# A decoder layer with routed experts on one core: the split of the groups into phases, the order of the attention units, and the dependencies of the result loads

## The chip, the cores and the metric

The kernel runs on one NeuronCore of one Trainium2 chip. The metric is the device time of one execution in microseconds (us). The profile is one execution taken by the hardware profiler. Engines are named as in its rows: PE (TensorE), PEld (TensorE weight loads), DVE (VectorE), ACT (ScalarE), POOL (GpSimd), SP (SyncE, which here only issues DMAs). "SPq" is SP's instruction queue.

## The reference

Input: `x` and `ctx_1024`, both [32, 128, 128] in float32 (32 sequences, 128 tokens, width 128), 16 heads of 8. One decoder layer:

```python
x = _layernorm(x + _attn(x, x, x, sa_..., True), ln1_g, ln1_b)        # causal self attention
x = _layernorm(x + _attn(x, enc, enc, ca_..., False), ln2_g, ln2_b)   # cross attention
x = _layernorm(x + _moe(x, router_w, router_b, e_w1, e_b1, e_w2, e_b2), ln3_g, ln3_b)
```

`_moe` takes the softmax of 8 router logits for each of the 4096 tokens, keeps the best two, softmaxes those two probabilities again, and adds the two experts' outputs with these weights. An expert is 128 -> 512, exact GELU, 512 -> 128.

## The kernel before, in words

**Groups and units.** The 32 sequences form 8 groups of G = 4. A unit is one sequence's self attention ("s") or cross attention ("c"), so there are 64. The list `order` (from L986) runs them in one software pipeline: 12 s units lead (LEAD), then c and s alternate, then 12 c units end it. Each unit takes two half-slots of its own and is spread over the next six: scores and row maxima (L456, L464), transposed scores and exponentials (L449, L472), values (L511), outputs (L525 to L530).

**The planner.** Everything else that a group needs is cut into generators that stop at `yield`: projections, normalisation (L323), hand-over to cross attention, `keep_x2`, `route` (L607), `place` and `biases`. From L1066 on each step gets a half-slot by hand-written costs (`ROUTE`, `PLACE`, `NORM`); `chain(lo, hi, ...)` puts steps into the least loaded half-slot of an interval and crams what is left into its last ones. The table is then played half-slot by half-slot, and each engine runs its instructions in that order.

**Routing.** `route` computes the logits (L614), subtracts the row maximum (L619), takes the exponential on ACT (L620), finds the best two (L629, L632), and takes a tanh on ACT (L637). `place` gives every token two rows in the table `xs` of its phase, sorted by expert into blocks of 128. `scatter` sends rows: one indirect DMA on POOL for one sequence and one choice (L760), 8 for a group, one for each half-slot; for the last group one for every second half-slot.

**Phases and blocks.** `PHASES` (L25) splits the groups: a phase's blocks can start when all its groups have been scattered. A phase of n groups has 8 blocks with a fixed expert and (1024 n - 8) // 128 whose expert is known at run time: 47 blocks for five groups and 31 for three, 78 in all. The blocks start at half-slot `max(behind, ready)`: `behind` is the end of the attention, 132, and `ready` the end of the first phase's scatters. From then on one half-slot of what is left in the table is played beside each block (`beside`). By the planner's rules, before: group 4 is scattered in half-slots 122 to 129, group 5 in 136 to 143 (blocks 4 to 11), group 6 in 144 to 151, group 7 in every second one from 152 to 166 (blocks 20 to 34). With a limit of h2 + 14 for the last group of the first phase, six of its seven projection and normalisation steps stand in half-slot 109, and nine steps of the last s group stand in half-slot 111.

**A block** (`Pipeline.run`, L928): SP loads the weights of the block four ahead (L825 or L829, 514 KB, five buffers); PE does the first layer (L864, 8 instructions), then the second layer of the block before (L880, 8 instructions); ACT does four GELUs (L869); DVE copies the result to `ot` (L885, four buffers); POOL scatters it into `eo` by an indirect DMA (L887). Every four blocks SP fetches a quad of rows (L812), PE transposes it (L841), DVE copies it (L856). The first quad of the second phase is fetched when the quad before is turned and waits for all scatters of that phase.

**Results.** `combine` (L948) of a group needs the scatters of the first 15, 23, 31, 39 or 47 blocks of its phase (`needed`) and starts four blocks later: at blocks 19, 27, 35 and 43 of the first phase and block 4 of the second for its five groups, at 19 and 27 of the second phase, and after the last block. It loads the base (L953) and the results `gt` (L955) on SP, yields twice (one yield is one block), adds with weights on DVE (L968), normalises and stores (L981). Two groups can be in work at a time. The line `for j in phases[p].done[: needed(...)]` ties the load to the scatters it needs. Whatever else wrote `eo` before the load in program order is tied to it as well, because the tile framework sees one tensor; and every later scatter is tied to the load. `tc.declare_no_dep` takes such a tie away, and is used between the scatters.

Of the kernel before, what the change touches and what calls it, by code (L numbers as in the profile page):

```python
# [21 lines left out]
FF = 512  # L22
NFC = FF // P
G = 4
PHASES = ((0, 5), (5, 3))  # L25
NP = len(PHASES)
NS = E

# [10 lines left out]
VS = 2 * VW  # L39
NPART = 3  # L40
LEAD = 12

TAG = P
XW = P + 2
# [8 lines left out]
def bc(ap, axis, n):  # L53

    ap = ap.unsqueeze(axis)
    shape = list(ap.shape)
    shape[axis] = n
    return ap.broadcast_to(shape)
# [3 lines left out]
def kernel(  # L62
# [35 lines left out]
    B = x.shape[0]  # L98
    NG = B // G
# [32 lines left out]
    groups = {(kind, gi): Group(kind, gi) for kind in "sc" for gi in range(NG)}  # L132
# [109 lines left out]
    lng, lnb, lngT, lnbT, later = [], [], [], [], {}  # L242
# [364 lines left out]
    def route(gr):  # L607


        gi = gr.gi  # L610
        bs = slice(G * gi, G * gi + G)
        pl = mm_tile([P, G, E], f"pl_{gi}")
        for b in range(G):
            nc.tensor.matmul(pl[:, b, :], lhsT=gr.x2T[:, b, :], rhs=rw, start=True, stop=True)  # L614
        lg = small.tile([P, G, E], F32, tag="lg", name=f"lg_{gi}")
        nc.vector.tensor_tensor(lg, pl, bc(rb, 1, G), ALU.add)
        lm = small.tile([P, G], F32, tag="lm", name=f"lm_{gi}")
        nc.vector.tensor_reduce(lm, lg, AX.X, ALU.max)
        nc.vector.tensor_tensor(lg, lg, bc(lm, 2, E), ALU.subtract)  # L619
        nc.scalar.activation(lg, lg, AF.Exp)  # L620
        yield
        ls = small.tile([P, G], F32, tag="ls", name=f"ls_{gi}")
        nc.vector.tensor_reduce(ls, lg, AX.X, ALU.add)
        nc.vector.reciprocal(ls, ls)
        nc.vector.tensor_tensor(lg, lg, bc(ls, 2, E), ALU.mult)
        top = small.tile([P, G, E], F32, tag="top", name=f"top_{gi}")
        idx = small.tile([P, G, E], U32, tag="idx", name=f"idx_{gi}")
        for b in range(G):
            nc.vector.max(top[:, b, :], lg[:, b, :])  # L629
        yield  # L630
        for b in range(G):
            nc.vector.max_index(idx[:, b, :], top[:, b, :], lg[:, b, :])  # L632


        ex = small.tile([P, G], F32, tag="ex", name=f"ex_{gi}")
        nc.vector.tensor_tensor(ex, top[:, :, 0], top[:, :, 1], ALU.subtract)
        nc.scalar.activation(ex, ex, AF.Tanh, scale=0.5)  # L637
        yield
        idf = small.tile([P, G, 2], F32, tag="idf", name=f"idf_{gi}")
        nc.vector.tensor_copy(idf, idx[:, :, 0:2])  # L640
        nc.vector.tensor_copy(gr.x2[:, :, TAG + 1], idf[:, :, 0])
        gr.onehot = small.tile([P, 2, G, E], F32, tag="onehot", name=f"onehot_{gi}", bufs=2)
        for k in range(2):
            nc.vector.tensor_tensor(
                gr.onehot[:, k], bc(later["iota_e"], 1, G), bc(idf[:, :, k], 2, E), ALU.is_equal
            )
        gr.chosen = small.tile([P, G, E], BF16, tag="chosen", name=f"chosen_{gi}", bufs=2)
        nc.vector.tensor_tensor(gr.chosen, gr.onehot[:, 0], gr.onehot[:, 1], ALU.add)
        yield
        nc.vector.tensor_scalar(wts[:, 0, bs], ex, 0.5, 0.5, ALU.mult, ALU.add)  # L650
        nc.vector.tensor_scalar(wts[:, 1, bs], ex, -0.5, 0.5, ALU.mult, ALU.add)


    class Phase:
# [4 lines left out]


        def __init__(self, p):
            self.p, self.sent, self.done, self.first = p, [], [], True

    phases = [Phase(p) for p in range(NP)]

# [130 lines left out]
    class Blocks:  # L796
# [76 lines left out]
        def second_layer(self, i):  # L873
            if i < 0:
                return
            q, p = i // XB, self.ph.p
            w, h = self.w.pop(i), self.h.pop(i)
            po = mm_tile([P, P], f"po_{p}_{i}")
            for c in range(NFC):
                nc.tensor.matmul(  # L880
                    po, lhsT=h[:, c, :], rhs=w[:, W2 + c * P : W2 + (c + 1) * P],
                    start=c == 0, stop=c == NFC - 1,
                )
            ot = moe.tile([P, P], F32, tag="ot", name=f"ot_{p}_{i}", bufs=4)
            nc.vector.tensor_copy(ot, po)  # L885
            nc.gpsimd.memset(apart, 0.0)
            s = nc.gpsimd.indirect_dma_start(  # L887
                out=eo[p][:, :],
                out_offset=bass.IndirectOffsetOnAxis(
                    ap=self.to[q][:, i % XB : i % XB + 1], axis=0  # L890
                ),
                in_=ot, in_offset=None,
            )
            for j in self.ph.done:
                tc.declare_no_dep(s.ins, j.ins, reason="rows of their own")
            self.ph.done.append(s)

# [46 lines left out]
    def needed(n):  # L944

        return NS + 2 * G * (n + 1) - 1

    def combine(gr):  # L948

        p = next(p for p, (g0, n) in enumerate(PHASES) if gr.gi < g0 + n)  # L950
        first = FREE[p] + 2 * P * G * (gr.gi - PHASES[p][0])
        gr.acc = moe.tile([P, G, P], F32, tag="acc", name=f"acc_{gr.gi}")
        nc.sync.dma_start(out=gr.acc, in_=x2d[gr.gi])  # L953
        gt = act.tile([P, 2, G, 2 * P], F32, tag="qb", name=f"gt_{gr.gi}", bufs=4)[:, 0]
        i = nc.sync.dma_start(  # L955
            out=gt,
            in_=eo[p][first : first + 2 * P * G, :].rearrange(
                "(p b k) d -> p b (k d)", p=P, k=2
            ),
        )  # L960
        for j in phases[p].done[: needed(gr.gi - PHASES[p][0])]:
            tc.add_manual_dep(i.ins, j.ins.name, SYNC, reason="results")
        yield
        yield
        for k in range(2):
            for b in range(G):
                t = G * gr.gi + b
                nc.vector.scalar_tensor_tensor(  # L968
                    gr.acc[:, b, :], gt[:, b, P * k : P * k + P], wts[:, k, t : t + 1],
                    gr.acc[:, b, :], ALU.mult, ALU.add,  # L970
                )
            yield
        yield from finish(gr)
# [9 lines left out]
        )  # L983


    order = []  # L986
    for j in range(B + LEAD):
        if j >= LEAD:
            order.append(("c", j - LEAD))
        if j < B:  # L990
            order.append(("s", j))
    units = [Unit(groups[kind, j // G], j % G) for kind, j in order]
    where = {(kind, j): t for t, (kind, j) in enumerate(order)}
    table = {}
# [1 line left out]
    def at(h, *call):  # L996
        table.setdefault(h, []).append(call)
        return h + 1
# [27 lines left out]
    def chain(lo, hi, *parts):  # L1026


        todo = []
        for made, *costs in parts:  # L1030
            if len(costs) == 1:
                todo.append((costs[0], (made,)))
                continue
            steps = []

            def step(made=made, steps=steps):
                if not steps:
                    steps.append(made())
                next(steps[0], None)

            todo += [(cost, (step,)) for cost in costs]
        ends = []
        for n, (cost, call) in enumerate(todo):
            left = len(todo) - 1 - n
            end = book(lo, hi - left, cost, *call)
            lo = end if hi - end + 1 >= left else end - 1
            ends.append(end)
        return ends

    def pe(us, act=0.0, dve=0.0):  # L1050
        return us, dve, act, 0.0

    def dve(us, act=0.0):
        return 0.0, us, act, 0.0
# [4 lines left out]
    NORM = (dve(1.2), (0.0, 0.9, 0.0, 1.3), dve(0.2), dve(0.0, 0.7), dve(0.0, 0.7))  # L1059
    TURN = (pe(0.45, 0.4),) * 2  # L1060
    PROJECT = (pe(0.45, 0.0, 0.4),) * 2
    ROUTE = (pe(0.3, 0.1, 0.9), dve(1.2), dve(1.1), dve(0.8), dve(0.4))
    PLACE = (pe(0.2, 0.0, 1.0), pe(0.3, 0.0, 0.8), dve(1.6), dve(0.8), dve(0.6))
    behind = 2 * (len(units) + 2)
    sent = 0
    for gi in range(NG):  # L1066
        s, c = groups["s", gi], groups["c", gi]
        h0, h3 = 2 * where["s", G * gi], 2 * where["s", G * gi + G - 1]
        h1, h2 = 2 * where["c", G * gi], 2 * where["c", G * gi + G - 1]
        if gi > 1:  # L1070
# [24 lines left out]
        )  # L1095
        chain(h1 - 1, h1 + 4, (lambda c=c: values_of(c), *TURN))
        ends = chain(
            h2 + 9, h2 + (14 if gi == PHASES[0][1] - 1 else 18),
            (lambda c=c: turn_output(c), *TURN),
            (lambda c=c: project(c), *PROJECT, *NORM),  # L1100
            (lambda c=c: keep_x2(c), *TURN, pool(1.3), pool(1.4)),
        )
        ends = chain(ends[10], ends[10] + 4, (lambda c=c: route(c), *ROUTE))
        ph = phases[next(p for p, (g0, n) in enumerate(PHASES) if gi < g0 + n)]
        ends = chain(ends[-1], ends[-1] + 4, (lambda c=c, ph=ph: place(c, ph), *PLACE))
        h = ends[3]
        chain(h, h + 5, (lambda c=c: biases(c), dve(0.6), pe(0.1, 0.3), pe(0.45, 0.0, 0.6), pool(0.0)))

        h, far = max(h, sent), 1 + (gi == NG - 1)
        for b in range(G):  # L1110
            for k in range(2):
                at(h, scatter, c, ph, b, k)
                h += far
        sent = h
        if gi == PHASES[0][1] - 1:
            ready = h
# [5 lines left out]

    blocks = Pipeline(*(Blocks(ph) for ph in phases))
    start = max(behind, ready)
    at(start - 3, blocks.prepare)
    at(start - 1, blocks.first_rows)

    def unit(t):
# [125 lines left out]
```

## Time and profile before

| | us |
|---|---|
| three runs | 720.62, 730.99, 732.46 (median 730.99) |
| the profiled execution | 720.12 |
| its span | 718.4 |
| attention, to the first block's first layer (L864) | 0 to 477.3 |
| blocks 0 to 77, to the end of the last second layer | 477.3 to 692.7 |
| tail | 692.7 to 718.4 |

Busy over the span: PE 594.3 us (83%), PEld 500.2, DVE 416.3, ACT 403.4, POOL 367.2. Such a share is an average over the two parts; what binds is read part by part. In a line of the timeline the first number is the start, the second the length, `xN` the number of instructions merged, and the bracket the idle time of the engine before it and what ended that. A line of waits has the total, the number of times and the longest. A line of the windows has, after the stretch, the busy time (and instructions) of PE, PEld, DVE, ACT and POOL, the granted PE clock (1.00 is full), the busy share of the 16 DMA engines and GB/s.

### The profile page before, as it was taken

The numbers are of one execution on the slowest core, as the hardware profiler recorded it, in microseconds if no ns is written. First come the engines' busy times: TensorE is split into PE (matmuls) and PEld (weight loads), VectorE is DVE, ScalarE is ACT, GpSimd is POOL, SyncE is SP. The second block draws the span as 40 slices with busy tenths as digits, with TensorE's granted clock in tenths as the row PEclk, the third lists the DMA queues.
The fourth block names the chain that finished last, engine by engine and source line by source line (L and its number), as shares of the span: only waits on it lengthen the run. The fifth ranks groups of instructions, "written<-read, shape, count | busy, mean of one in ns | idle before, by whom it ended". The sixth has DMA issues, their size and how long they took to land. (4 is left out here: it accounts for less than half of the span.)

```text
span 718.4 us, 21892 instructions
## 1 busy us (share of the span) xinstructions
PE 594.3 (83%) x8810; PEld 500.2 (70%) x8863; DVE 416.3 (58%) x1321; ACT 403.4 (56%) x919; POOL 367.2 (51%) x747
## 2 busy tenths in 40 slices
PE   8787999999897987987987888998986697699750
PEld 6565677777775776766776667777885697599750
DVE  2555465656786777678678577436674424353343
ACT  4455666776764683684576554354843454266441
POOL 3274654544446636646554453514886565265350
PEclk9999999999998998998999899759998988799985
DMA  5012516400000200100100000415996889699851
GB/s 133 19 33 64 86 44 192 170 4 17 16 3 17 62 2 14 50 2 24 35 21 6 13 30 10 156 60 173 302 296 227 265 291 313 228 353 346 274 181 59
DMA packets 48038, 82.48 MB, mean 115 GB/s; under 512 B 7968, under 2 KB 26464, under 8 KB 47936
## 3 DMA queue, kind: packets, MB, share of 16 engines
q1 hardware_dynamic: 42816, 71.57, 31.6%
q0 software_dynamic: 4544, 9.38, 3.6%
q8 instruction: 69, 1.13, 0.6%
q14 instruction: 33, 0.27, 0.1%
q10 hardware_dynamic: 576, 0.13, 0.1%
HBM read 62.15 MB, written 23.10 MB: 119 GB/s over the span
## 5 line engine op out<-in xcount | busy, mean ns | idle before, releaser
L869 ACT ACTIVATE h<-ph,wd 128x128 f32<-128x128 f32 x312 | 88.9, 369 | 86.4 <-PE ph L864 46.6
L887 POOL DMA_INDIRECT eo<-ot,to x78 | 78.1, 1001 | 98.3 <-DMA gt<-eo 34.9
L864 PE MATMUL ph<-xT,wd 128*128 128x128 f32 x624 | 93.2, 297 | 32.6 <-DMA wd<-wpk 12.5
L464 DVE TENSOR_REDUCE m_s<-sc_s 128x8 f32<-128x1024 f32 x64 | 78.3, 1223 | 67.1 <-PE st_s L449 59.1
L476 POOL TENSOR_SCALAR_AFFINE_SELECT pr_s<-pr_s 128x1024 f32<-128x1024 f32 x64 | 70.1, 1095 | 86.3 <-ACT pr_s L472 86.1
L864 PEld LDWEIGHTS ph<-xT,wd 128*128 128x128 f32 x624 | 84.4, 210 | 37.4 <-DVE xT L856 15.0
L464 DVE TENSOR_REDUCE m_c<-sc_c 128x8 f32<-128x1024 f32 x64 | 78.3, 1223 | 46.4 <-PE st_c L449 28.8
L472 ACT ACTIVATE pr_s<-st_s 128x1024 f32<-128x1024 f32 x64 | 65.8, 1028 | 65.0 <-PE st_s L449 64.9
L472 ACT ACTIVATE pr_c<-st_c 128x1024 f32<-128x1024 f32 x64 | 65.8, 1029 | 60.7 <-PE st_c L449 58.1
L456 PE MATMUL sc_c<-k_c,qb_c 32*128 32x128 f32 x1024 | 80.1, 297 | 14.0 <-DVE m_s L464 9.0
L880 PE MATMUL po<-wd,h 128*128 128x128 f32 x624 | 87.8, 286 | 1.1 <-ACT h L869 1.1
L880 PEld LDWEIGHTS po<-wd,h 128*128 128x128 f32 x624 | 81.1, 202 | 1.8 <-ACT h L869 1.5
L449 PE MATMUL st_c<-qb_c,k_c 32*128 32x128 f32 x1024 | 77.8, 291 | 0.0
L456 PEld LDWEIGHTS sc_c<-k_c,qb_c 32*128 32x128 f32 x1024 | 67.0, 198 | 15.3 <-DVE m_s L464 9.6
L449 PEld LDWEIGHTS st_c<-qb_c,k_c 32*128 32x128 f32 x1024 | 76.2, 205 | 0.9
L456 PE MATMUL sc_s<-k_s,qb_s 32*128 32x128 f32 x1024 | 74.2, 283 | 0.3
L760 POOL DMA_INDIRECT xs<-x,slots x64 | 64.4, 1007 | 12.0 <-issue 12.0
L449 PEld LDWEIGHTS st_s<-qb_s,k_s 32*128 32x128 f32 x1024 | 67.7, 187 | 0.0
L449 PE MATMUL st_s<-qb_s,k_s 32*128 32x128 f32 x1024 | 67.4, 270 | 0.0
L456 PEld LDWEIGHTS sc_s<-k_s,qb_s 32*128 32x128 f32 x1024 | 62.1, 185 | 1.7 <-issue 1.3
L885 DVE COPY ot<-po 128x128 f32<-128x128 f32 x78 | 22.5, 288 | 60.1 <-PE po L880 46.6
L441 PEld LDWEIGHTS <-ones 32*128 32x128 bf16 x256 | 14.8, 91 | 56.8 <-issue 54.8
(243 smaller groups left out, 1220.1 us busy)
## 6 DMA issues: line engine op xcount, KB each, us to landing
wd<-wpk SPq DMA_DIRECT2D x78, 514.0 KB, 5.4
xt<-xs SPq DMA_DIRECT2D x20, 260.0 KB
wpk<-in_L_xattn_e_w_dram SPq DMA_DIRECT2D x16, 256.0 KB, 6.4
gt<-eo SPq DMA_DIRECT2D x8, 512.0 KB
xs<-blank SPq DMA_DIRECT2D x1, 3120.0 KB
xs<-blank SPq DMA_DIRECT2D x1, 2080.0 KB
xg<-in_x_dram SPq DMA_DIRECT2D x8, 256.0 KB, 3.2
eg<-in_ctx_dram SPq DMA_DIRECT2D x8, 256.0 KB, 7.2
```

The costliest lines, as they stand in the source:

```text
L441: nc.tensor.matmul(st[:, i], lhsT=ones16[rowsof(g), :], rhs=old.mq[rowsof(g)], start=True, stop=False,)
L449: nc.tensor.matmul(st[:, i, r, :], lhsT=old.group.k[rowsof(g), old.b, :], rhs=old.group.qb[rowsof(g), old.b, r, :], start=False, stop=r == 3,)
L456: nc.tensor.matmul(sc[:, i, r, :], lhsT=new.group.qb[rowsof(g), new.b, r, :], rhs=new.group.k[rowsof(g), new.b, :], start=not new.masked, ...
L464: nc.vector.tensor_reduce(new.m[:, 8 * half : 8 * half + 8], sc.rearrange("p i r k -> p (i r) k"), AX.X, ALU.max,)
L472: nc.scalar.activation(old.pr[:, hs, :], st.rearrange("p i r k -> p (i r) k"), AF.Exp, scale=SCALE)
L476: nc.gpsimd.affine_select(out=old.pr[:, hs, :], in_=old.pr[:, hs, :], pattern=[[0, 8], [1, P]], compare_op=ALU.is_ge, fill=0.0, base=0, ch ...
L760: i = nc.gpsimd.indirect_dma_start(out=xs[ph.p][:, :], out_offset=bass.IndirectOffsetOnAxis(ap=slots[:, k, t : t + 1], axis=0), in_=gr.x2[ ...
L864: nc.tensor.matmul(hid[:, c, :], lhsT=w[:, c * P : (c + 1) * P], rhs=self.xT[i // XB][:, i % XB, :], start=True, stop=True,)
L869: nc.scalar.activation(self.h[i][:, c, :], hid[:, c, :], AF.Gelu, bias=w[:, B1 + c : B1 + c + 1])
L880: nc.tensor.matmul(po, lhsT=h[:, c, :], rhs=w[:, W2 + c * P : W2 + (c + 1) * P], start=c == 0, stop=c == NFC - 1,)
L885: nc.vector.tensor_copy(ot, po)
L887: s = nc.gpsimd.indirect_dma_start(out=eo[p][:, :], out_offset=bass.IndirectOffsetOnAxis(ap=self.to[q][:, i % XB : i % XB + 1], axis=0), i ...
```

## The change

- Phases of four and four groups instead of five and three: 39 and 39 blocks, still 78.
- The order of units: at s units 16, 20 and 24 no c unit is put in between, so that self attention runs up to 15 units ahead and 15 c units end the list.
- The limit h2 + 14 becomes h2 + 18 for all groups; the last group's scatters stand in every half-slot.
- `route` yields once more, before the exponential, and the tanh moves behind its yield (so each is issued one step after the DVE work that it reads); one step more in `ROUTE`.
- The load of a group's results is declared free of the scatters behind the ones it needs, and later scatters are declared free of the loads. After the load there are four yields instead of two.
- The first four weight loads are issued six half-slots ahead of the blocks instead of three.

```diff
-PHASES = ((0, 5), (5, 3))
+PHASES = ((0, 4), (4, 4))
+MORE = (16, 20, 24)
...
         nc.vector.tensor_tensor(lg, lg, bc(lm, 2, E), ALU.subtract)
+        yield
         nc.scalar.activation(lg, lg, AF.Exp)
         yield
...
         nc.vector.tensor_tensor(ex, top[:, :, 0], top[:, :, 1], ALU.subtract)
+        yield
         nc.scalar.activation(ex, ex, AF.Tanh, scale=0.5)
-        yield
...
-            self.p, self.sent, self.done, self.first = p, [], [], True
+            self.p, self.sent, self.done, self.loads, self.first = p, [], [], [], True
...
-            for j in self.ph.done:
+            for j in self.ph.done + self.ph.loads:
                 tc.declare_no_dep(s.ins, j.ins, reason="rows of their own")
...
-        for j in phases[p].done[: needed(gr.gi - PHASES[p][0])]:
+        n = needed(gr.gi - PHASES[p][0])
+        for j in phases[p].done[:n]:
             tc.add_manual_dep(i.ins, j.ins.name, SYNC, reason="results")
-        yield
-        yield
+        for j in phases[p].done[n:]:
+            tc.declare_no_dep(i.ins, j.ins, reason="rows of later groups")
+        phases[p].loads.append(i)
+        for _ in range(4):
+            yield
...
-    order = []
-    for j in range(B + LEAD):
-        if j >= LEAD:
-            order.append(("c", j - LEAD))
-        if j < B:
-            order.append(("s", j))
+    order = [("s", j) for j in range(LEAD)]
+    for j in range(LEAD, B):
+        if j not in MORE:
+            order.append(("c", sum(kind == "c" for kind, _ in order)))
+        order.append(("s", j))
+    order += [("c", j) for j in range(len(order) - B, B)]
...
-    ROUTE = (pe(0.3, 0.1, 0.9), dve(1.2), dve(1.1), dve(0.8), dve(0.4))
+    ROUTE = (pe(0.3, 0.0, 0.9), dve(0.0, 0.2), dve(1.2), dve(1.1), dve(0.8), dve(0.4))
...
-            h2 + 9, h2 + (14 if gi == PHASES[0][1] - 1 else 18),
+            h2 + 9, h2 + 18,
...
-        ends = chain(ends[10], ends[10] + 4, (lambda c=c: route(c), *ROUTE))
+        ends = chain(ends[10], ends[10] + 5, (lambda c=c: route(c), *ROUTE))
...
-        h, far = max(h, sent), 1 + (gi == NG - 1)
+        h = max(h, sent)
         for b in range(G):
             for k in range(2):
                 at(h, scatter, c, ph, b, k)
-                h += far
+                h += 1
...
-    at(start - 3, blocks.prepare)
+    at(start - 6, blocks.prepare)
```

## The prediction

> **What bounds the kernel now.** I read the page first, then the windows, the waits of the second half, and the timelines of SP, POOL and PE around one wait.
>
> ```profile
> PEclk9999999999998998998999899759998988799985
> DMA  5012516400000200100100000415996889699851
> L887 POOL DMA_INDIRECT eo<-ot,to x78 | 78.1, 1001 | 98.3 <-DMA gt<-eo 34.9
> L864 PE MATMUL ph<-xT,wd 128*128 128x128 f32 x624 | 93.2, 297 | 32.6 <-DMA wd<-wpk 12.5
> ```
>
> There are two halves. Up to slice 26 the DMA engines are nearly idle and PE is busy some 86% (attention). From slice 27 on (the blocks) DMA is at 0.6 to 0.9 and the PE clock dips. Of POOL's scatters of results, 34.9 us of idle time ended with a load of results.
>
> ```profile
> POOL eo L887 <- DMA gt<-eo: 34.9, 5, 9.4
> DVE acc L968 <- DMA gt<-eo: 37.5, 8, 6.5
> SPq L955 <- DMA eo<-ot,to: 41.4, 8, 8.7
> ```
>
> This is a ring: the load waits on SP for the newest scatter (41.4 us, 8 times), later scatters wait on POOL for the load, and DVE waits for it in `combine`. One case, on SP, POOL and PE:
>
> ```profile
> 534.85 0.44 SPq L953 DMA_DIRECT2D acc<-x2d  x1
> 544.18 0.33 SPq L955 DMA_DIRECT2D gt<-eo  x1
> 545.43 2.67 SPq L829 DMA_DIRECT2D wd<-wpk  x3
> ```
> ```profile
> 531.66 0.97 POOL L887 DMA_INDIRECT eo<-ot,to  x1 [0.22 <-issue]
> ...
> 541.85 0.97 POOL L887 DMA_INDIRECT eo<-ot,to  x1 [0.23 <-DVE sums L746]
> ...
> 548.74 1.05 POOL L887 DMA_INDIRECT eo<-ot,to  x1 [4.56 <-DMA gt<-eo]
> ```
> ```profile
> 551.31 2.05 PE L864 MATMUL ph<-xT,wd 128*128 128x128 f32 x8 [5.08 <-DMA wd<-wpk]
> 553.14 1.77 PE L880 MATMUL po<-wd,h 128*128 128x128 f32 x8
> 554.75 1.06 PE L864 MATMUL ph<-xT,wd 128*128 128x128 f32 x8
> ```
>
> Counting POOL's scatters from 484.74 (block 0), 531.66 is scatter 14, the last that the group needs, and 541.85 is scatter 18. SP could have issued the load at about 536.5 (531.66 plus the median 4.6 to landing) and did at 544.18, when scatter 18 had landed. Three weight loads queued behind it, PE ran dry for 5.08 us, and its next block took 3.44 us (551.31 to 554.75) instead of 1.79, since the clock had dropped.
>
> **The change part by part.** The sum is made against the profiled execution (span 718.4, 1.7 around it).
>
> *1. Loads free of later scatters.* The price before, for each of the seven loads inside the block loop, is PE idle plus what the next blocks take over 1.79 us: 6.7 (load at 544.2), 6.7 (567.7), 7.3 (591.0), 9.5 (614.2), 1.5 (634.0), 6.3 (670.7). At the seventh (689.9) PE has done; its last scatter leaves at 698.56, though the second layer ended at 692.67 and a copy and an issue take under 1 us: 5.1. Together 43. Not all of it comes back: other limits take over, so I go by stretches.
>
> *2. Attention.* The number of half-slots stays 132. Crammed half-slots go (109 and 111); around them, from 392 to 418 us, PE's timeline shows gaps of 2.10, 0.94, 0.52, 1.34 and 2.13 us and one half-clock stretch of 6.8, in which 3.4 are lost. Against that, the planner now has more slots with over 3.6 us on one engine. I take -4, from -9 (nearly all of these 10.4) to +6 (two more of the gaps of 3 us that PE has once a group, at 218, 277 and 335 us). Buffers for s groups that run further ahead stay in number by the planner's slots; no price, and if one is short, one gap of the 3 us kind.
>
> *3. Exponential a step later.* At block 3, ACT loads its table at 489.28, waits 2.25 us for DVE's L619 and only then copies the outputs that PE needs: PE idles 3.14 us (to 493.35) and then runs about 1.7 slow. With the exponential a step later the copies go first; two table loads of 1.28 then stand between GELUs, which cost PE 1.11 us at 519.03. Net -3, from -5 to 0. The later step moves place and scatter by one half-slot: nothing, since POOL lags anyway (next).
>
> *4. POOL's stretch.* From scatter 3 (498.44) on POOL never rests: pairs of result and row scatter follow each other in 2.54 us (529.11, 531.66, 534.21), longer than PE's 1.79. Before, row scatters stand at each of the blocks 4 to 19, then at every second one to 34. After, group 4 fills half-slots 129 to 136, and groups 5 to 7 137 to 160: one at each block up to 28. Result scatters 3 to 28 then take 25 x 2.54 = 63.5, plus `keep_x2` and normalisation in POOL's rows (5.4 + 1.3): 70.2 us against 75.8 before (498.44 to 574.27), with two waits for loads (4.56 and 6.03) gone. So -5.6, and not -10.6: the denser row scatters take 5 back. Five row scatters of group 4 come to blocks 0 to 4; POOL idles 1.15, 2.32 and 5.70 us there, which covers 5 x 1.27; if that cover is gone, +6.4.
>
> *5. Blocks 33 to 77.* At the end of the stretch PE is 5 blocks ahead (scatter 18 at 541.85, first layer 23 at 543.23), so block 33 starts 1.4 us behind scatter 28, not 3.6 as before: -2.2. Then 45 blocks took 114.8 us before. Undisturbed, blocks 49 to 70 (626.88 to 670.27) took 2.07 us each with one load of results among 21; PE alone needs 1.90 with its transposes. A block moves 514 KB of weights, 65 of rows and 64 of results, and one `combine` in eight blocks 1,024 KB. These blocks have five, and I take 2.17, between 2.07 and 2.29 (for 21 blocks 1.7 MB more than then, 4.7 us at the 360 GB/s of 640 to 665 us). That is 97.7, plus 1 us for each load of results (its own scatter is five blocks old, 10 us, where landing takes 4.6): 102.7, so -12.1. Ends: 45 x 1.90 = 85.5, and 115 if nothing is won.
>
> ```profile
> 645.00:650.00 5.00, 4.69 (x42) 4.49 (x41) 1.72 (x8) 3.42 (x12) 4.12 (x8) 1.00 1.02 405
> 460.00:480.00 20.00, 18.40 (x172) 14.88 (x175) 6.65 (x44) 7.68 (x13) 5.85 (x14) 0.50 0.33 116
> ```
>
> The first row is the fastest stretch of DMA: 405 GB/s, so 34.9 MB for these blocks would pass in 86 us. The Trainium skill ("DMA: Bandwidth & Descriptors", Specifications) states a limit of about 358 GB/s of HBM for a core, which would speak against the change, since it makes the transfers the floor at 97 us; the row exceeds it for 5 us, and no row shows more than 360 held for 25.
>
> *6. Four yields, and the tail.* The load has 8.7 us (four blocks) instead of 4.3 before DVE asks; issue to use took 3.3 to 4 us, more behind queued weights (5.4 to land). The DVE wait of 37.5 goes inside the loop; if a load needs 9 us, each costs 1. At the end, 5.1 us of late scatters go; but the group before last now does its sums in the tail, and the last base load waits for a buffer whose store leaves later (4.2 us now, L953), so I give 3 back: -2.2, from -5 to +3.
>
> *7. Costed at nothing.* Weight loads three half-slots earlier: they pass one store of a base on SP, at DMA shares under 0.3, and land long before 477; that store now stands behind them, before block 7's weights; as group 5's does today (508.26) with no gap on PE. The first rows of phase two are fetched at block 34 instead of 42 and wait for row scatters that end with block 28 on POOL; four blocks of weights (7.6 us) cover that; without it, up to 4.
>
> Sum: -4 - 3 - 5.6 - 2.2 - 12.1 - 2.2 = -29.1. Span 689.3, time 691.0. The median of the three runs stands 10.9 above the profiled 720.1, the lowest at 720.6. A median after may stand on either level; I add 4: **695**.
>
> **The rivals.**
> - *The transfers bind.* For: DMA share 0.86 and 298 GB/s over 575 to 690 already. Against: 405 for 5 us. Then part 5 stays at 2.55 us a block: 695 + 12 = 707.
> - *The load still waits, for its own scatters.* For: POOL is five blocks behind when its stretch ends. Against: it needs 1.27 a block from block 29 on, while PE takes 2.1. Half of the price at six loads (3 each, 18, of which 5 are in the sum): 708.
> - *The ties stay* (the change doesn't do what it says): parts 2 and 3 remain, -7, and the denser scatters cost 6: about 723.
> - *Slower: the half clock in the c units at the end.* 460 to 480 ran at 0.50 with PE busy, 172 instructions where the 20 us before had 312: what takes 1 us takes 1.81. For: the run of c units, with fewer matmuls per slot, grows from 24 half-slots to 30 (about 105 us). Against: from 400 to 457 the clock fell for only 3 to 7 us at a time. It undoes the gain from 36 us of work on; with 66 of the 105, +53: 748. The Trainium skill ("TensorE: Matmul & The Clock Gate", What's actually happening) says that about 3.4 us of sustained work restores the clock, which would exclude this; the row above, busy for 20 us at 0.50, contradicts it, so I keep the rival.
>
> **How the numbers follow.** Forecast 0.64; transfers 0.17; own scatters 0.10; ties 0.04; half clock 0.05. The forecast's own range is 677 to 709. The low end 676 takes attention at -9, 2.03 us a block and no waits at the loads (-5, -6, -5, and 3 of the 4 added for the median); the high end 716 takes in both rivals at 707 and 708 with attention at +4. I measure against 731, where 2% (716 to 745) is about what runs of this spread can tell. Faster 0.83 (the first three cases, 0.91, less 0.08 for those of them that meet a bad attention), same 0.13 (those and the ties), slower 0.04.
>
> **What would show it.** Right: no wait of POOL's L887 for `gt`; SP's wait at L955 under 10 us in all but the last; no PE gap of over 3 us after block 5; scatters 3 to 28 in 70 us; the last second layer 24 us ahead of now. Wrong: PE waiting for `wd` at 300 GB/s (transfers), POOL busy beyond block 33, or DVE's L968 waiting for `gt` as before.

## The result, and the profile after

The changed kernel took 683.13 us (median of 4 runs, 682.63 to 688.0), the kernel before beside it 727.29 (4 runs, 720.62 to 732.46). The ratio is 0.944, interval 0.934 to 0.954: faster. Forecast: 695, between 676 and 716. A second set of runs of the same changed kernel on another chip gave 658.65 beside 725.17, ratio 0.912 (0.905 to 0.919), which is below that range. So one question is what differs between two profiles of one kernel.

| stage (us) | before | predicted | after, 1st profile | after, 2nd profile |
|---|---|---|---|---|
| attention, to block 0 | 477.3 | 473.3 | 458.9 | 447.5 |
| block 0 to POOL's result scatter 3 | 21.1 | 18.1 | 19.7 | 18.3 |
| scatter 3 to 28 | 75.8 | 70.2 | 82.2 | 70.5 |
| scatter 28 to block 33 | 3.6 | 1.4 | 3.9 | 1.5 |
| block 33 to the last second layer | 114.8 | 102.7 | 96.0 | 96.3 |
| tail | 25.8 | 23.6 | 20.6 | 20.4 |
| span | 718.4 | 689.3 | 681.4 | 654.5 |

The page of the first profile after; its first two rows are 40 slices of the span:

```profile
PEclk9699999899999999999999999998968899999995
DMA  6010701731010020001001000604667889999972
...
L889 POOL DMA_INDIRECT eo<-ot,to x78 | 78.5, 1007 | 66.2 <-DVE acc L974 15.0
...
L866 PE MATMUL ph<-xT,wd 128*128 128x128 f32 x624 | 89.5, 289 | 9.3 <-DMA wd<-wpk 3.8
```

The clock is at 9 over the last third, and DMA at 9 for slices 33 to 37. PE's idle time before first layers fell from 32.6 to 9.3 us. No wait of POOL's scatters for a load of results is left. The waits of the ring, all of them, in the same profile:

```profile
SPq L957 <- DMA eo<-ot,to: 1.1, 3, 0.7
...
DVE acc L974 <- DMA gt<-eo: 2.3, 1, 2.3
```

Before they were 41.4 and 37.5. The ring is gone. In the stretch from scatter 3 to 28 stands something that no row of before shows (timeline of the first profile after):

```profile
534.14 1.06 PE L866 MATMUL ph<-xT,wd 128*128 128x128 f32 x8
...
535.03 1.06 PE L882 MATMUL po<-wd,h 128*128 128x128 f32 x8
...
539.75 1.14 ACT L871 ACTIVATE h<-ph,wd 128x128 f32<-128x128 f32 x4 [5.40 <-issue]
...
541.25 1.50 SPq L831 DMA_DIRECT2D wd<-wpk  x2
541.25 0.29 DVE L887 COPY ot<-po 128x128 f32<-128x128 f32 x1 [4.60 <-PE po L882]
```

PE's first layer ends at 535.2 by the model, yet its GELU starts at 539.75, after a wait for nothing that the profile shows; the copy of a second layer that ends at 536.1, and the weight load that needs its buffer, start together at 541.25. I call these late signals. Three engines pay at once, and PE's granted clock is 0.5 for 6.8 us from 540.1. The ends of matmuls are modelled, so the trace can't tell whether the signal was late or the matmul itself was held. As a measure I take ACT's idle time before GELUs that the profile puts to "issue".

### The profile page after: what moved, and what is told of

It is laid out like the page before. It is cut to its first block, busy times and chain, and to the rows that moved or that the text cites. A ratio compares the mean times of both kernels' runs of the same rounds, so it can differ in the third digit from the quotient of the medians.

```text
span 681.4 us, 21953 instructions
## 1 busy us (share of the span) xinstructions
PE 591.5 (87%) x8863; PEld 486.6 (71%) x8863; DVE 409.2 (60%) x1321; ACT 402.4 (59%) x919; POOL 368.0 (54%) x747
## 4 chain that ended last, share of the span: by engine, by line
PE 59%; DVE 16%; ACT 9%; issue 6%; DMA 6%; POOL 3%; SPq 1%; ACTq 0%; DVEq 0%; another core or an unknown queue 0%; POOLq 0%
PE ph L866 7%; PE po L882 7%; PE st_s L450 6%; PE st_c L450 5%; PE sc_s L437 4%; DVE m_s L465 4%; DMA wd<-wpk 4%; PE po_s L512 3%; DVE m_c L465 3%; PE po_c L512 3%; PE sc_c L457 3%; PE st_s L442 2%; ACT pr_s L473 2%; PE st_c L442 2%; PE sc_s L457 2%
## 5 line engine op out<-in xcount | busy, mean ns | idle before, releaser
L871 ACT ACTIVATE h<-ph,wd 128x128 f32<-128x128 f32 x312 | 88.0, 371 | 79.1 <-issue 45.6
L465 DVE TENSOR_REDUCE m_c<-sc_c 128x8 f32<-128x1024 f32 x64 | 78.0, 1219 | 32.6 <-PE st_c L450 19.6
L866 PE MATMUL ph<-xT,wd 128*128 128x128 f32 x624 | 89.5, 289 | 9.3 <-DMA wd<-wpk 3.8
L866 PEld LDWEIGHTS ph<-xT,wd 128*128 128x128 f32 x624 | 80.6, 202 | 15.2 <-issue 6.3
L457 PE MATMUL sc_c<-k_c,qb_c 32*128 32x128 f32 x1024 | 75.3, 283 | 4.5 <-DVE m_c L465 4.1
L457 PE MATMUL sc_s<-k_s,qb_s 32*128 32x128 f32 x1024 | 78.1, 293 | 0.0
L450 PE MATMUL st_c<-qb_c,k_c 32*128 32x128 f32 x1024 | 70.2, 272 | 0.2 <-issue 0.2
L450 PE MATMUL st_s<-qb_s,k_s 32*128 32x128 f32 x1024 | 69.6, 275 | 0.0
L450 PEld LDWEIGHTS st_c<-qb_c,k_c 32*128 32x128 f32 x1024 | 68.8, 187 | 0.9 <-issue 0.4
L457 PEld LDWEIGHTS sc_s<-k_s,qb_s 32*128 32x128 f32 x1024 | 65.5, 194 | 2.5 <-issue 2.1
L457 PEld LDWEIGHTS sc_c<-k_c,qb_c 32*128 32x128 f32 x1024 | 62.5, 185 | 6.1 <-DVE m_c L465 5.7
L437 PE MATMUL sc_s<-causal,ident 128*128 128x512 bf16 x128 | 39.7, 393 | 13.7 <-DVE m_s L465 10.3
```

Source lines behind the costliest of these rows:

```text
L437: nc.tensor.matmul(sc[:, i], lhsT=ident16, rhs=causal, start=True, stop=False)
L450: nc.tensor.matmul(st[:, i, r, :], lhsT=old.group.k[rowsof(g), old.b, :], rhs=old.group.qb[rowsof(g), old.b, r, :], start=False, stop=r == 3,)
L457: nc.tensor.matmul(sc[:, i, r, :], lhsT=new.group.qb[rowsof(g), new.b, r, :], rhs=new.group.k[rowsof(g), new.b, :], start=not new.masked, ...
L465: nc.vector.tensor_reduce(new.m[:, 8 * half : 8 * half + 8], sc.rearrange("p i r k -> p (i r) k"), AX.X, ALU.max,)
L866: nc.tensor.matmul(hid[:, c, :], lhsT=w[:, c * P : (c + 1) * P], rhs=self.xT[i // XB][:, i % XB, :], start=True, stop=True,)
L871: nc.scalar.activation(self.h[i][:, c, :], hid[:, c, :], AF.Gelu, bias=w[:, B1 + c : B1 + c + 1])
```

## The experiments

Twelve runs in four sets, each with the kernel before beside it. The sets ran on different chips. All kernels of the first set, and the first profile after, show late signals (45.6 to 83.6 us of that ACT wait), and no kernel of the other sets does (14.5 to 25.4; before 21.2). So stages are compared within a set, or between profiles without late signals. Attention is counted here from the first self unit's transposed scores (L449 of before), since some profiles start 3 to 6 us later; the table above counts from the start of the span.

| kernel | set | us | ratio to before (interval) | attention | 3 to 28 | 33 on | ACT wait |
|---|---|---|---|---|---|---|---|
| before, first profile | - | | | 454.8 | 75.8 | 114.8 | 21.2 |
| after, first profile | - | 683.1 | 0.944 (0.934-0.954) | 433.0 | 82.2 | 96.0 | 45.6 |
| after, ties kept | 1 | 706.1 | 0.969 (0.941-0.996) | 431.3 | 92.1 | 111.0 | 45.7 |
| before + free loads | 1 | 700.8 | 0.962 (0.944-0.979) | 453.7 | 76.2 | 100.2 | 47.8 |
| before + exponential | 1 | 723.5 | 0.989 (0.982-0.997) | 447.4 | 86.0 | 117.3 | 83.6 |
| before + order | 1 | 735.6 | 1.013 (0.992-1.033) | 458.4 | 87.0 | 117.0 | 77.8 |
| before | 2 | 726.3 | 1.005 (0.997-1.012) | 456.3 | 75.7 | 115.8 | 21.2 |
| before + phases | 2 | 715.7 | 0.994 (0.986-1.002) | 446.5 | 77.7 | 114.9 | 18.8 |
| after, old order | 2 | 658.6 | 0.906 (0.895-0.916) | 424.0 | 69.2 | 95.3 | 16.1 |
| after, old exponential | 2 | 674.9 | 0.935 (0.927-0.942) | 439.6 | 69.1 | 96.1 | 21.8 |
| after | 3 | 658.7 | 0.912 (0.905-0.919) | 424.9 | 70.5 | 96.3 | 19.7 |
| after, old order, two yields | 3 | 663.5 | 0.917 (0.909-0.925) | 422.0 | 69.8 | 103.3 | 25.4 |
| after, weights 3 ahead | 3 | 678.9 | 0.935 (0.927-0.944) | 427.0 | 70.6 | 115.1 | 14.5 |
| after, old order, again | 4 | 652.3 | 0.901 (0.896-0.907) | 422.2 | 69.3 | 94.1 | 18.5 |

**Set 1: one part at a time.** At 2% three of the four ratios of this set (0.969, 0.962, 1.013) are unclear and the fourth (0.989) is "same", so the set is read by its stages. The changed kernel with the ties:

```diff
-            for j in self.ph.done + self.ph.loads:
+            for j in self.ph.done:
...
-        for j in phases[p].done[n:]:
-            tc.declare_no_dep(i.ins, j.ins, reason="rows of later groups")
-        phases[p].loads.append(i)
```

> The changed kernel with its loads of results tied to all scatters of their phase again; phases, order of units, the exponential's step and the four yields stay as changed. My theory (the ties make a ring of SP, POOL and DVE that costs PE some 3 to 7 us a load): blocks 33 to the last second layer take 111 to 117 us (96.0 in the changed kernel, 114.8 before), PE has gaps of 3 to 5 us after loads again, and the stretch from scatter 3 to 28 gains 3 to 8 us for its two loads; in all 18 to 26 us above the changed kernel, 702 to 709. Rival A (the gain after block 33 comes from the phases of four and four, which leave fewer loads and row scatters there): blocks 33 on stay within 96 to 100 us and the time within 683 to 690. Rival B (with the ties kept nothing of the change remains but the attention): as before less 18, 709 to 713.

Measured 706.1, as my theory had it (702 to 709). Blocks 33 on took 111.0, at the edge of what my theory asked (111 to 117), and the waits are back:

```profile
POOL eo L889 <- DVE acc L971: 44.0, 11, 8.6
...
PE ph L866 <- DMA wd<-wpk: 18.1, 7, 4.7
...
DVE acc L971 <- DMA gt<-eo: 9.1, 5, 3.6
```

SP's wait at the load is 33.1 us again. Rival A falls: the phases don't make the gain after block 33. Now the same part alone, on the kernel before (the free loads and four yields of the diff, nothing else).

> The kernel before with the loads of results freed from later scatters and four yields in place of two, and nothing else of the change. My theory: attention as before (477 us to block 0), blocks 33 on take 96 to 103 us instead of 114.8, the stretch of scatters 3 to 28 loses the two waits for loads (4.56 and 6.03), the tail 2 to 5: 22 to 30 us off in all. Rival (with phases of five and three the loads come late and together, so that the transfers of five groups' results bind): 10 to 15 us off. Rival (the loads are free but wait for their own scatters): SP still waits 20 us or more at the load, 12 to 18 us off.

0.962, which is 28 us off the 731 of before beside it (my theory: 22 to 30), with SP's wait at the load 1.0 us in all and blocks 33 on 100.2. Both rivals fall. What missed is the stretch from 3 to 28, which lost nothing (76.2): in this set it carries late signals. The two other parts alone:

```diff
         nc.vector.tensor_tensor(lg, lg, bc(lm, 2, E), ALU.subtract)
+        yield
         nc.scalar.activation(lg, lg, AF.Exp)
...
         nc.vector.tensor_tensor(ex, top[:, :, 0], top[:, :, 1], ALU.subtract)
+        yield
         nc.scalar.activation(ex, ex, AF.Tanh, scale=0.5)
-        yield
...
+    ROUTE = (pe(0.3, 0.0, 0.9), dve(0.0, 0.2), dve(1.2), dve(1.1), dve(0.8), dve(0.4))
```

> The kernel before with the routing's exponential (and its Tanh) a step later, as the change has it, and nothing else of it. My theory: 3 us off (0 to 5), all in blocks 0 to scatter 3, where PE no longer waits 3.14 us beside ACT's wait for DVE; attention as before (475 to 478 us). Rival A (each route held ACT long enough to open a gap on PE in attention, and the gap a stretch at half clock): attention falls by 8 to 18 us and its time at half clock from 55.8 us to under 30. Rival B (the longer chain of a step per group moves later work into fuller slots): 0 to 4 us more.

> The kernel before with the order of the attention's units changed (three slots with a self unit alone, three more cross units alone at the end), and nothing else. My theory, as predicted: 4 us off attention (between 9 off and 6 more). Rival A (the order is what took 18.4 us from attention, by ridding it of the gaps of about 3 us once a group after which the clock is halved for 6.8): attention 459 to 463 us, half clock there under 30 us instead of 55.8. Rival B (the cross units at the end fall to half clock for longer, as from 459 to 483 before): half clock at the end of attention over 30 us, and 5 to 15 us more.

Up to block 0 the kernel with free loads plays as before does, so its attention, 453.7, is this set's measure. The exponential alone: block 0 to scatter 3 fell from 21.1 to 17.9 as predicted, but attention fell too, by 6.3, though this part was costed at nothing there. Rival A asked for 8 to 18 and for under 30 us at half clock; it has 38.1. The order alone: attention 458.4, 4.7 longer, and the fall to 35.8 us at half clock bought nothing. Rival B isn't met either (17.1 us of half clock at the end, not over 30). With the new order alone PE stood idle for 6.30 us at the end of attention, before the first rows:

```profile
478.78 1.09 PE L842 MATMUL px<-ident,xt 128*128 128x128 f32 x4 [6.30 <-DMA xt<-xs]
```

My -4 and rival A both fall: the order isn't what shortened attention.

**Set 2: what shortened attention.** The kernel before, and with the phases alone (with the limit, the row scatters at every half-slot and the weight loads that belong to them); the changed kernel with the old order, and with the old step of the exponential. The edits are the hunks of the diff, taken or taken back.

> The kernel before, unchanged: a second profile of it. The profile shown of before is of its fastest execution (720.1, where the median of the runs is 731 to 733). Theory A (the longer stretch of scatters 3 to 28 in the changed kernel and in all four experiments that lengthen it is a hold-up of the chip that the first profile happened to miss: PE's signals reach ACT, DVE and SP 3 to 7 us late at single places): this profile is at 728 to 740, scatters 3 to 28 take 82 to 90 us instead of 75.8, and ACT's wait before the GELU that the profile puts to no releaser comes to 40 to 80 us instead of 21.2. Theory B (the changes themselves lengthen it): 75 to 77 us and 20 to 25 us again.

> The kernel before with phases of four and four groups and what goes with them (the same limit for every group's chain, row scatters at every half-slot, weight loads three half-slots earlier), and nothing else of the change. My theory: the shorter limit of the first phase's last group was what crammed the end of attention; attention falls by 6 to 12 us (465 to 471 to block 0), blocks 33 on stay at 108 to 116 since the ties stay; 8 to 16 us off in all. Rival A (as predicted for that part): attention 3 to 5 us off, the rest within 3 us. Rival B (phases alone bring nothing in attention; the 18 us come only together with the order or the exponential): attention 475 to 479.

> The changed kernel with the order of the units as before. Theory A (the order brings nothing, as it did alone): attention 456 to 462, time 680 to 688. Theory B (the order brings its gain only where the phases no longer cram the chains): attention 466 to 475 and 7 to 16 us more. Rival C (the order costs by itself, as it did alone): 3 to 6 us less than the changed kernel.

> The changed kernel with the routing's exponential at its step of before. Theory A (it is worth in the changed kernel what it was alone): attention 464 to 468 (7 more), block 0 to scatter 3 2 to 3 us more, 8 to 11 us more in all. Theory B (alone it only moved later work out of crammed slots, which the phases also do): attention 457 to 462, 2 to 4 us more in all, from the blocks. Theory C (the exponential and the order need each other): 12 us or more.

The second profile of before has its stretch at 75.7 and ACT's wait at 21.2: as the first, with 726.8 us. So late signals aren't what makes it slower than the 720 of the first profile, and Theory A fails for this chip; but three changed kernels had none here either, and their stretch is 69.1 to 77.7. Theory B, that the changes make them, fails with that too.

Attention, within the set: phases 456.3 to 446.5, -9.8 (my theory). In time the phases alone can't be told from before (0.994, "same", where my theory had 8 to 16 us off), so this part rests on the profiles. With the exponential's step as well (and the free loads, which do nothing before block 0) 424.0, another -22.5. That is the part that I had missed. PE's waits from 200 to 360 us, phases alone:

```profile
PE sc_c L456 <- DVE m_s L464: 8.9, 3, 3.1
```

and the changed kernel with the old order:

```profile
PE sc_c L456 <- DVE m_s L464: 1.2, 3, 0.7
```

Three gaps of 3 us, one a group, each followed by 6.8 us at half clock (3.4 lost): 19 by this count. What opens them, in the timeline of phases alone:

```profile
220.87 1.23 POOL L760 DMA_INDIRECT xs<-x,slots  x1 [0.19 <-issue]
...
221.46 3.04 DVE L746 TENSOR_TENSOR sums<-sums,part 128x31 f32<-128x31 f32 x1
...
222.13 1.27 POOL L572 TENSOR_TENSOR x<-x,lnb1c 128x512 f32<-128x512 f32 x1
...
223.35 1.09 POOL L476 TENSOR_SCALAR_AFFINE_SELECT pr_s<-pr_s 128x1024 f32<-128x1024 f32 x1
...
226.46 0.58 PE L456 MATMUL sc_c<-k_c,qb_c 32*128 32x128 f32 x2 [3.06 <-DVE m_s L464]
```

DVE's sum of 31 columns, 0.19 us in the median, lasts 3.04: from POOL's row scatter to the end of the mask at 224.44. Behind it on DVE stand the normalisation and the row maxima that PE waits for. With the exponential one step later, `place` ends one half-slot later, and its sum doesn't meet this row of POOL work: 0.25, 0.20 and 0.20 us at 230.4, 282.7 and 334.8 in the changed kernel with the old order. The Trainium skill ("SBUF — State Buffer", Who interferes with whom) says that a DVE instruction with two SBUF inputs contends with a GpSimd instruction that reads SBUF, since its second input comes through a shared read interface. These rows agree, with 3.04 us against 0.19. They add that the wait can last over several POOL instructions in a row. With the exponential alone the three gaps go in the same way (1.2, 3, 0.7).

The gaps aren't the whole of the 22.5, though. Both kernels play the matmuls of the values (L511) in one order, and by their starts the changed kernel with the old order gains 15.8 us between 198 and 360: 1.9, 4.6 and 4.5 at the three gaps (in the first group a new wait of 1.80 for `m_c`, at 216.96, takes part of it back), and 1.3 once a group where, with the phases alone, ACT's tanh stands for 1.3 us until DVE's L636 is done and PE waits for ACT (`st_c` for `pr_c`, 3.8 us, 3 times). The other 6.7 lie outside this stretch and weren't followed.

In the new order, which is that of the change, the step is worth 14.7 (439.6 to 424.9; in all the kernel with the old exponential is 16 us slower than the changed kernel of set 3, the size of Theory C), and mostly by another road. Only one of its sums lasts long (3.03 us, at 219.92), and 9.5 of the 14.7 come after 379 us. The largest piece there is what the prediction had seen at block 3: ACT stands at the exponential until DVE is ready, and the copy that PE needs waits behind it.

```profile
443.06 0.23 ACT L621 ACTIVATE lg<-lg 128x32 f32<-128x32 f32 x1 [3.57 <-DVE lg L620]
443.20 0.63 ACT L542 COPY oT_c<-to_c 128x256 f32<-128x256 f32 x2
443.61 2.08 PE L551 MATMUL py_c<-woc,oT_c 128*128 128x128 f32 x8 [3.54 <-ACT oT_c L542]
```

These are lines of the changed kernel with the old exponential. PE's granted clock is 0.5 there from 442.5 to 466.4; the changed kernel has 13.7 us of half clock at the end of attention instead of 23.9.

The old order beat the changed kernel's first result by far, more than any of my three theories allowed: 0.906. Most of that isn't the order's: without late signals the changed kernel itself takes 658.7 (set 3).

**Set 3: the changed kernel again, yields, and how far ahead weights are fetched.**

> The changed kernel, unchanged: a second profile of it, to see whether its scatters 3 to 28 (82.2 us, predicted 70.2) are so long by the change or by the place it ran. Theory A (ACT, DVE and SP saw PE's signals 4 to 5 us late there, as in the four experiments of the first set, and none did in the second set): without late signals this stretch takes 68 to 72 us, ACT waits under 5 us before GELUs for a signal that PE's rows show as long given, and the time is 668 to 676; with them again, 80 to 86 us and 680 to 690. Theory B (the six units moved by the new order make it long, since the kernel without the order has 69.2): 80 to 84 us with ACT's late signals at 5 us or less.

Theory A. Without late signals the stretch is 70.5, the predicted 70.2 plus 0.3, and the kernel is even better than Theory A had it: 658.7. The waits didn't fall under Theory A's 5 us, though (8.9). ACT's waits inside this stretch, first profile after:

```profile
ACT h L871 <- issue: 32.1, 12, 5.4
```

and second:

```profile
ACT h L871 <- issue: 8.9, 6, 2.4
```

The old order with two yields (`range(2)` for `range(4)`):

> The changed kernel with the order of the units as before, and with two yields between a load of results and its use in place of four; the rest as changed. Theory A (the load lands in 4 to 5.4 us, two blocks are 4.2, so DVE waits about a us a load and PE is ahead of it): within 3 us of the kernel without the order alone, ratio to before 0.90 to 0.912. Theory B (DVE waits long enough to hold up the copies that PE and POOL need, as before): DVE waits 15 us or more at the sums for the load, blocks 33 on take 100 to 104 us instead of 95.3, ratio 0.913 to 0.925.

Theory B: DVE waits for every load, and blocks 33 on take 103.3 in place of 95.3 and 94.1.

```profile
DVE acc L973 <- DMA gt<-eo: 22.9, 8, 4.2
```

Weights three blocks ahead (`AHEAD = 3`):

> The changed kernel with weights fetched three blocks ahead instead of four (one buffer less). Theory A (the late signals stand beside full DMA, when several loads of 514 KB are under way at once): with three ahead the late signals fall to a half or less of what the changed kernel shows in the same set, and scatters 3 to 28 are shorter by 3 to 10 us if it shows any. Theory B (the loads are what bounds the blocks, and each needs its four blocks): PE waits for weights 10 us or more in all, and the time is 5 to 15 us longer than the changed kernel's in the same set. Theory C: neither, within 3 us.

Theory B, above its range: 20 us more than the changed kernel in the same set.

```profile
PE ph L866 <- DMA wd<-wpk: 28.0, 26, 2.6
```

Late signals didn't occur in this set, so the run says nothing on their cause. But it shows how near the transfers are. The windows of blocks 33 on, second profile after (DMA share and GB/s are the last two columns):

```profile
538.00:570.00 32.00, 29.40 (x255) 28.49 (x254) 16.48 (x69) 19.78 (x70) 20.48 (x37) 1.00 1.01 356
570.00:602.00 32.00, 29.43 (x257) 28.80 (x256) 13.89 (x58) 18.88 (x66) 17.78 (x34) 1.00 0.99 363
602.00:634.00 32.00, 29.96 (x259) 29.32 (x259) 16.14 (x67) 19.82 (x68) 19.12 (x35) 1.00 0.90 336
```

and with weights three ahead, the first of its windows:

```profile
545.00:583.00 38.00, 29.41 (x238) 28.23 (x237) 16.31 (x69) 18.93 (x65) 19.49 (x36) 0.96 0.90 304
```

With four ahead DMA runs at a share of 1.00 for 64 us and PE is busy 92% of the time (29.4 of 32). With three it is 0.90 and 77%.

**Set 4: the old order again.**

> The changed kernel with the order of the units as before, a second time, with more rounds, since its ratio (0.9056) stands beside the changed kernel's second one (0.9118) from another set. Theory A (the new order costs some 5 us, 2.8 in attention and 2.2 up to scatter 3, as the profiles of the third set show): ratio to before 0.900 to 0.908, scatters 3 to 28 in 69 to 71 us, blocks 33 on in 95 to 97, block 0 at 444 to 447 (or 450 to 453 with the slow start of some profiles). Theory B (no difference in the end): 0.909 to 0.916. With late signals of PE, as in the first set: scatters 3 to 28 in 78 to 84 us, ratio 0.92 to 0.94; if this order keeps them away, as Theory C has it, there are none in any set.

Theory A: 0.901, and no late signals (blocks 33 on, 94.1, just under its 95). In the profiles of sets 3 and 4 the old order reaches block 0 earlier by 2.3 us, scatter 3 by 4.5 and the end by 5.7 (span 648.8 against 654.5). It is the best version here, 72 us under before beside it. Its interval ends at 0.907 and that of the changed kernel begins at 0.905, from another chip, so a gain of 1% over the changed kernel is likely and not proven.

## Why the prediction was right or wrong

The direction, the mechanism of the main part and the number held on the first measurement. That the number came so near was in part luck: two misses of opposite sign helped, since attention gave 14 us more than the sum had, and the stretch with the late signals took 12 back. Without late signals the sum (-29.1) is less than half of what came (-63.9 of span), and the time, 658.7, is under the low end of the range, 676, which took attention at -9.

1. *Loads free of later scatters: right.* The signs named for it are all there (no POOL wait for `gt`, SP's waits 1.1 us). Kept ties cost 15 us after block 33 and 4 in the tail within otherwise the same kernel.
2. *Attention, "I take -4": wrong, -18.4 in the first profile and -29.8 in the second.* The crammed half-slots were sized well at "nearly all of these 10.4" and too low at -4: the phases with their limit gave -9.8. The rest came from a part that I had costed for one place only.
3. *Exponential, "Net -3": right at its place alone, wrong in its reach.* On the kernel before it took 3.2 off the stretch from block 0 to scatter 3. The changed kernel gained 2.8 there, but with the old exponential it has 18.7 in place of 18.3, so there the step itself is worth 0.4. And the step sits in every group's chain: -22.5 in attention with the old order, -14.7 with the new (439.6 to 424.9). I had the gaps at 218, 277 and 335 on the page, used them as a price for harm, and never followed one back to the 3 us DVE row beside POOL's scatter. I also wrote that the step "moves place and scatter by one half-slot: nothing": with the old order that move closed the three gaps, 11.0 of the 22.5. And ACT's wait for DVE, which I had priced at block 3 alone, stood at other groups' routing as well; with the new order that and the half clock behind it are the largest piece found (6.2 of the 14.7, from 436 to 456 us).
4. *POOL's stretch, 70.2: right where no signals are late* (70.5, 69.2, 69.3, 69.1). There POOL does not rest: its waits before scatters are 0.2 us each but for one of 1.7. In the first profile it was 82.2, and I had no row for that. Its cause is open.
5. *Blocks 33 on, 102.7: too long by 6.* A block took 2.13 to 2.14 us, loads of results included, where I had 2.17 and "1 us for each load" (5). That us is real with two yields (103.3) and gone with four. Scatter 28 to block 33: 1.5 in the second profile, as predicted (1.4); 3.9 in the first.
6. *Tail, -2.2: -5.2.* The 3 us given back for a later base store weren't taken.
7. *Costed at nothing:* weight loads six half-slots ahead left no gap on PE before block 8; right.

The rivals. *Transfers bind* was right in part, and wrong in its price: DMA is full from block 33 on, but at 2.13 us a block and not 2.55, since the earlier profile's 298 GB/s was what the ring let through. PE is as near its own limit: in the second profile it is busy for 89 of these 96 us, and 3.4 of its idle 7 are waits for weights. The Trainium skill's limit of about 358 GB/s of HBM for a core ("DMA: Bandwidth & Descriptors", Specifications), which I set aside for one row of 405 over 5 us, gives an estimate of 97 us for these blocks. They took 94 to 96, at 360 over 95 us (windows of the first profile: 376, 361, 341), so the trace agrees, though its first 32 us are above the page's figure. *Own scatters*: no, SP waits 1.1 us. *Ties stay*: no. *Half clock at the end of attention*: 6.8 and 13.7 us of it in the two profiles after, against 23.9 before, and 23.9 again with the old exponential; it never reached the length that decides.

What stays open is why signals are late on some chips. The rate of the transfers doesn't explain it: DMA moved 302 GB/s over this stretch without them (second profile) and 241 with them (first), and the 64 us at a share of 1.00 in the second profile had none.

## What to carry to other kernels

A gap that recurs once a group is worth following through the waiting engine's queue to the long row before it; ask then of every moved step whether it moves that row, too. A wait that is found at one place of a repeated step should be looked for at all its others. When a ring of waits is taken out, size the result by the transfer rate that was held at full share over tens of us, and not by a rate that was measured inside the ring. And take the profile of both kernels twice, on different chips, before a stage that grew is explained by the change.

## What the runs showed of the hardware that was not expected

- A DVE addition of 128 x 31 elements took 3.0 us beside three POOL instructions in a row (2.9 for the 128 x 39 of before), and 0.19 in the median; in before and in the kernel with the phases alone each such case cost PE 3 us idle and 3.4 of the 6.8 us at half clock after it. Shorter rows of POOL work made it 1.2 to 1.9, and in all 26 cases over 1 us, in all traces here, it ended within 0.1 us after a POOL instruction did.
- In the first set and in the first profile after, ACT, DVE and SP at times went on 4 to 5 us after the modelled end of the matmuls that they waited for, all three at about the same moment (539.75 to 541.25). In the first profile after, four GELUs of blocks 16 to 27 started 2.6 to 5.2 us late, and the stretch with them is 11.7 us longer than without (82.2 against 70.5). Attention is 8.1 us longer there as well (433.0 against 424.9); for what reason was not followed up.
- With weights fetched three blocks ahead instead of four (514 KB less on their way), the time rose by 20 us from 659: PE waited 28.0 us for weights in 26 places, and DMA moved 304 GB/s where it had moved 356.
